# A two-layer kernel on one core: W2's first half through a split, a quarter of the up weights through an adding DMA, and one whole last store

## The chip, the core and the metric

The kernel runs on one core of a Trainium2 chip. The engines that matter are TensorE (PE, with its weight loads shown as PEld), VectorE (DVE), ScalarE (ACT), GpSimd (POOL) and SyncE (SP), which here only issues DMAs. The time is the device time of one execution in microseconds (us). Three runs of the kernel before gave 359.22, 359.46 and 359.85, so its median is 359.46 us.

## What is computed

The input x has 4 batches of 512 rows of 256 numbers, all in float32. Each of two layers does the same outer step with an inner pair of functions:

```
xn = layernorm(x);  s = mixer(xn);  g = silu(ffn(xn));  x = x + s * g

ffn(x):    up_gate = x @ W1.T;  up_lin = x @ W3.T          # W1, W3: 1024 x 256
           hidden  = fwht(silu(up_gate) * up_lin)          # Walsh-Hadamard over 1024, scaled
           return hidden @ W2.T                            # W2: 256 x 1024
mixer, layer 0: x + rmsnorm((g * (x @ W_in.T)) @ W_out.T) with one step of a recurrence from state zero
mixer, layer 1: causal attention with one head, then + x
```

The Hadamard transform is linear, so the kernel puts it on W2 once, and not on the hidden values of every batch.

## The kernel before

**Numbers in two parts.** A product of 512 columns in full float32 takes 0.86 us of PE here, one in float32r 0.233, so nearly all operands are split: a high part `hi` that float32r can hold, and the rest `lo`. `split` (L59 to L62) makes them with a copy on ACT and a subtraction, src minus hi, on DVE. `mm3` (L80) then needs three fast products for each full one: hi·lo, lo·hi and hi·hi.

**The weights of layer 0.** The up weights W1 and W3 come as four quarters of 512 KB, one tile of 128x1024 each. `load_w13` (L114) loads them by SP, and `split_w13` (L122) splits them; quarter 0 goes in two halves. Quarter q serves the hidden blocks 2q and 2q+1 of eight. W2 comes in two halves of 128x1024. `prep_w2` (L143) runs three butterfly stages on DVE (each is one addition and one subtraction of 128x512, L155 and L156), which do the Hadamard transform over the 8 blocks; a product with a 128x128 Hadamard matrix on PE does the rest, and its result in PSUM (`w2ps`) is split into `w2h` and `w2l`. The last butterfly result is split too, into `w2bh` and `w2bl`, and multiplied by `had`, the matrix in float32r, in four fast products. Half 0 of layer 0 is the exception ("native"): its last butterfly result goes to PE as full float32, in two products with the full float32 matrix `had_f`.

**Layer 0, batch by batch.** `ffn` (L466 to L561) takes hidden block c = 0 to 7 in turn: two groups of six products of 512 columns, the up-gate and up-linear parts `gu{c}_0` and `gu{c}_1` in PSUM; then a silu on ACT (L527) and a multiplication on DVE (L528, the "gate") give h; a split gives hh and hl. The down products (`dn`, 256 columns each) come later. In the first batch (`f0_0`), the high parts hh0 to hh3 are put into spare tiles (`early`), and the down products come after all the up products. The gu tiles rotate through a few PSUM banks, so a later group has to wait until silu and gate have read an earlier one.

**What stands beside it.** An object `Beside` (L884) gives out other work in slots of the batch's loop: for the first batch `prep_first` (L965: W2 of layer 0 and the product M of the mixer's two matrices, which scales `wout` into wgh and wgl, and splits `win`), then mixer and norm; for the second, W2 of layer 1 and the attention's weight products; for the third and fourth, the weights of layer 1 (`sraw` is loaded, combined, stored as `sw`, and loaded again) and the next norms. But this only says in which order the program is written. **The order on each engine in layer 0 is set by the tile framework's scheduler**, which moves independent instructions past each other from its own durations (L1197, `schedule_with_timeline_sim=True`), except where `issue_after` (`after(...)`, L463) ties one behind another. So an edit in one place can reorder all of layer 0. In layer 1 the order on PE is written out by hand (`line["fixed"]`, and the list `places` from L1083).

**Layer 1 and the end.** `ffn_s` (L563) does the same layer function with another scheme of half-size products. For the last batch, `gate_tile` (L1058) takes each of the four tiles of 128 rows as its down products end: silu on ACT, multiplication and addition on DVE (L1063, L1064), then a store. `first["last"]` ties the next tile's multiplication behind this tile's addition. Tiles 0 to 2 are stored whole by SP (L1066). Tile 3 is stored as 64 rows by SP and 64 rows by ACT (L1070).

The functions that the diff touches:

Of the kernel before, what the change touches and what calls it, by code (L numbers as in the profile page):

```python
# [11 lines left out]
F32 = mybir.dt.float32  # L12
# [9 lines left out]
P = 128  # L22
# [13 lines left out]
def kernel(ctx: ExitStack, tc: tile.TileContext, a: dict, out: bass.AP):  # L36
# [22 lines left out]
    def split(src, hi, lo, engine=nc.vector):  # L59

        h = nc.scalar.copy(hi, src)  # L61
        return h, engine.tensor_tensor(lo, src, hi.bitcast(F32), ALU.subtract)  # L62

    line = {"fixed": False, "last": None}
# [55 lines left out]
    def split_w13(layer, q, raw):  # L122
        both = wp.tile([P, 2, 2, S], F32R, tag="w13", name=f"w13_{layer}_{q}", bufs=4)
        hi, lo = both[:, 0], both[:, 1]
        if (layer, q) != (0, 0):
            split(raw, hi, lo)
            return hi, lo
        halves = [slice(c * D, (c + 1) * D) for c in range(2)]
        split(*(z[:, :, halves[0]] for z in (raw, hi, lo)))
        next(normed)  # L130
        with after(first["norm"][0]), after(first["norm"][1]):
            hi_, lo_ = split(*(z[:, :, halves[1]] for z in (raw, hi, lo)))
        first["w13"] = hi_, lo_
        return hi, lo
# [8 lines left out]
    def prep_w2(layer, raws, dst, scratch):  # L143

        w2h, w2l = dst
        for half in range(2):
            ds_ = slice(half * P, (half + 1) * P)
            cur = raws[half]  # L150
            for st, h in enumerate((1, 2, 4)):
                nxt = scratch(f"w2b{st}_{layer}_{half}", [P, NH, P])
                cv = cur.rearrange("p (g two h) d -> p g two (h d)", two=2, h=h)
                nv = nxt.rearrange("p (g two h) d -> p g two (h d)", two=2, h=h)
                nc.vector.tensor_tensor(nv[:, :, 0], cv[:, :, 0], cv[:, :, 1], ALU.add)  # L155
                nc.vector.tensor_tensor(nv[:, :, 1], cv[:, :, 0], cv[:, :, 1], ALU.subtract)  # L156
                cur = nxt
                yield

            native = layer == 0 and half == 0  # L160
            if not native:
                bh = t4(f"w2bh_{layer}_{half}", [P, NH, P], F32R)
                bl = t4(f"w2bl_{layer}_{half}", [P, NH, P], F32R)
                split(cur, bh, bl)
                yield
            for q in range(2):
                o = psum(f"w2ps_{layer}_{half}_{q}", [P, NH // 2, P])
                qs = slice(q * NH // 2, (q + 1) * NH // 2)
                if native:
                    matmul(o, had_f, cur[:, qs, :], start=True, stop=True)  # L170
                else:
                    matmul(o, had, bh[:, qs, :], start=True, stop=False)
                    matmul(o, had, bl[:, qs, :], start=False, stop=True)
                split(o, w2h[:, qs, ds_], w2l[:, qs, ds_])
                yield

# [289 lines left out]
    def ffn(name, xT, w13, w2, slot, defer=1, spare=(), parts=1, behind=False, tail=()):  # L466

        w2h, w2l = w2
        dn, outs, firsts = [], [], {}

        def down(c, hh, hl, tiles=range(NT)):
            if not dn:
                dn.extend(psum(f"{name}dn{i}", [P, 2, D], tag="dn", bufs=2) for i in range(2))
                outs.extend(dn[t // 2][:, t % 2, :] for t in range(NT))
            for t in tiles:
                o = outs[t]
                for n, (l, r) in enumerate(((hh, w2h), (hh, w2l), (hl, w2h))):  # L480
                    first = c == 0 and n == 0
                    stop = c == NH - 1 and n == 2

                    def one(start):
                        return matmul(
                            o, l[:, sl(t)], r[:, c, :], start=start, stop=stop, skip_group_check=True
                        )

                    if first and t % 2 == 1:
                        with tc.issue_after(firsts[t // 2].ins):
                            ins = one(False)
                    elif first:
                        ins = firsts[t // 2] = one(True)
                    else:
                        ins = one(False)
            return ins

        queue, gates, late = [], [], []  # L500
        for c in range(NH):
            with after(gates[-2] if behind and c >= 2 else None):
                wh, wl = w13(c // 2)
            gu = []
            for j in range(2):

                o = psum(f"{name}gu{c}_{j}", [P, S], **(DN[0] if behind and c == 1 else GU))
                cols = slice((c % 2) * D + j * P, (c % 2) * D + (j + 1) * P)
                gu.append((o, cols))
            for half in range(parts if c == 0 else 1):  # L510
                n = S // (parts if c == 0 else 1)
                ts_ = slice(half * n, (half + 1) * n)
                if parts == 1 or c:
                    for o, cols in gu:
                        last_up = mm3(o[:, ts_], k_pairs((wh, wl), cols, xT, ts_))
                    continue

                for n, (w, x) in enumerate(((wh, xT[0]), (wl, xT[0]), (wh, xT[1]))):
                    for o, cols in gu:
                        for k in range(2):  # L520
                            last_up = matmul(
                                o[:, ts_], w[:, k, cols], x[:, k, ts_],
                                start=n + k == 0, stop=n + k == 3,
                            )
            gu = [o for o, _ in gu]
            h = hid(f"{name}h{c}")
            first["silu"] = nc.scalar.activation(h, gu[0], AF.Silu)  # L527
            gates.append(nc.vector.tensor_tensor(h, h, gu[1], ALU.mult))  # L528
            first["gate"] = gates[-1]
            if c < len(spare):  # L530
                hh, hl = spare[c]
            else:
                hh = hid(f"{name}hh{c}", F32R)
                hl = hid(f"{name}hl{c}", F32R)
            if c < len(spare):
                nc.scalar.copy(hh, h)
                late.append((hl, h, hh))
            else:
                split(h, hh, hl)
            for _ in range(2 if c >= NH - 2 else 0):  # L540
                if late:
                    lo_, h_, hi_ = late.pop(0)
                    with after(gates[-1]):
                        nc.vector.tensor_tensor(lo_, h_, hi_.bitcast(F32), ALU.subtract)
            queue.append((c, hh, hl))
            ups = last_up if behind else None
            with after(gates[-1] if behind else None), after(ups):
                slot(2 * c)
            if len(queue) > defer:
                down(*queue.pop(0))  # L550
            with after(gates[-1] if behind else None), after(ups):
                slot(2 * c + 1)
        line["fixed"] = bool(tail)
        line["last"] = last_up
        for what in tail:
            what()
        for q in queue:

            with after(first.get("xt") if behind and q[0] >= NH - 2 else None):
                down(*q)  # L560
        return dn  # L561
# [403 lines left out]
    def prep_first():  # L965
        steps = prep_w2(0, raw2, w2, x_slot)
        with after(first["w13"][1]):
            next(steps)
        yield
        for _ in range(4):  # L970
            next(steps)
            yield
        with after(first["silu"]):
            nc.scalar.copy(had, had_f)
        for _ in range(2):
            next(steps)
            yield
        for _ in range(2):
            next(steps)
            yield  # L980
        load_x(1)
        product = prep_m(*raw_m)
        next(product)
        yield
        next(steps)
        yield
        next(product)
        yield
        yield from steps
# [68 lines left out]
    def gate_tile(t, o):  # L1058
# [2 lines left out]
        nc.scalar.activation(g, o, AF.Silu)  # L1061
        with after(first.get("last")):
            nc.vector.tensor_tensor(g, g, s, ALU.mult)  # L1063
        first["last"] = nc.vector.tensor_tensor(x, x, g, ALU.add)  # L1064
        if t + 1 < NT:
            nc.sync.dma_start(out[B - 1, sl(t), :], x)  # L1066
            return

        for queue, rows in ((nc.sync, slice(0, P // 2)), (nc.scalar, slice(P // 2, P))):
            queue.dma_start(out[B - 1, sl(t), :][rows], x[rows])  # L1070

    loaded = {}

# [127 lines left out]
```

## Time and profile before

| what | value |
|---|---|
| median of three runs | 359.46 us |
| the profiled execution's own time | 359.25 us |
| its span in the trace | 357.46 us (1.79 us lie outside) |
| PE busy | 350.7 us, 98% |
| PEld busy | 326.8 us, 91% |
| DVE busy | 287.2 us, 80% |
| ACT busy | 197.5 us, 55% |
| POOL busy | 20.8 us, 6% |
| first product of the up weights | 7.8 us |
| start of the last product | 352.21 us |
| last packet of the last store | 356.27 us |

The table's busy times come from the page of one profiled execution. A line of the timeline reads: start in us, length in us, engine, line, operation, out<-in, shape, number of instructions, and in brackets how long the engine was idle before it and who ended the wait. Instructions of one engine overlap by some 0.1 us in such lines: steps are therefore best measured from start to start. A product in full float32 shows as two records in the trace.

### The profile page before, as it was taken

To read this page: it belongs to the slowest core of one execution; us is meant where nothing else is said; L and a number is where in the kernel's file an instruction comes from. 1 tells how busy PE (TensorE), PEld (TensorE's weight loads), DVE (VectorE), ACT (ScalarE), POOL (GpSimd) and SP (SyncE) were. 2 spreads that over 40 slices of the span, in tenths; PEclk is the share of its full clock that TensorE was granted. 3 is DMA by queue.
4 is the path that set the end of the run, shared out by engine and by line. 5 is a ranking of instruction groups with operands and counts; after the bars stand their busy time and mean duration, and the time that the engine had idled before them with its cause. 6 is when DMAs were issued, how large, how long until landed. Compare 5 with 4: busy or idle time off the path is not lost.

```text
span 357.5 us, 6276 instructions
## 1 busy us (share of the span) xinstructions
PE 350.7 (98%) x2477; PEld 326.8 (91%) x2477; DVE 287.2 (80%) x597; ACT 197.5 (55%) x373; POOL 20.8 (6%) x22
## 2 busy tenths in 40 slices
PE   7999999999999999999999999999999999999994
PEld 5878998888988898888999999999999999999994
DVE  6899659998579938998887957989679897577645
ACT  4666166265463425674467745586455676555443
POOL 2000110300021110100100001100011000000000
PEclk9999999999999999999999999999999999999999
DMA  7935000301054316756257135662554635444401
GB/s 241 337 87 211 2 1 2 117 0 61 0 169 174 131 42 230 257 179 200 96 210 261 54 153 208 229 234 73 201 208 172 217 145 205 176 146 173 185 0 59
DMA packets 16300, 52.25 MB, mean 146 GB/s; under 512 B 1648, under 2 KB 7952, under 8 KB 16272
## 3 DMA queue, kind: packets, MB, share of 16 engines
q1 hardware_dynamic: 15904, 51.54, 40.9%
q8 instruction: 19, 0.31, 0.4%
q10 hardware_dynamic: 368, 0.33, 0.3%
q14 instruction: 9, 0.07, 0.1%
HBM read 42.40 MB, written 9.45 MB: 145 GB/s over the span
## 4 chain that ended last, share of the span: by engine, by line
PE 95%; DVE 3%; DMA 1%; ACT 0%; issue 0%; DVEq 0%
PE f_0dn L70 6%; PE f_1dn L70 6%; PE f_2dn L70 6%; PE f_0gu L70 6%; PE f_1gu L70 6%; PE f_2gu L70 6%; PE f_3gu L70 6%; PE f_3dn L70 5%; PE sc L70 4%; PE pv L70 4%; PE o L70 3%; PE v L70 3%; PE tq L70 3%; PE w2ps L70 1%; PE pt L70 1%; PE mps L70 1%
## 5 line engine op out<-in xcount | busy, mean ns | idle before, releaser
L70 PE MATMUL f_3gu<-xt,w 128*128 128x512 f32 x96 | 25.0, 396 | 0.0
L70 PE MATMUL f_2gu<-xt,w 128*128 128x512 f32 x96 | 24.8, 395 | 0.0
L70 PE MATMUL f_1gu<-xt,w 128*128 128x512 f32 x96 | 24.8, 395 | 0.0
L70 PE MATMUL f_0gu<-xt,w 128*128 128x512 f32 (+1 forms) x108 | 24.3, 378 | 0.0
L70 PEld LDWEIGHTS f_0gu<-xt,w 128*128 128x128 f32 x108 | 18.4, 188 | 4.6 <-issue 0.7
L70 PEld LDWEIGHTS f_1gu<-xt,w 128*128 128x128 f32 x96 | 17.0, 188 | 3.1
L70 PEld LDWEIGHTS f_2gu<-xt,w 128*128 128x128 f32 x96 | 17.0, 188 | 3.0
L70 PEld LDWEIGHTS f_3gu<-xt,w 128*128 128x128 f32 x96 | 17.0, 188 | 2.9
L61 ACT CAST f_2hh<-f_2h 128x512 fp32r<-128x512 f32 x16 | 10.0, 622 | 15.5 <-DVE f_2h L528 12.4
L70 PE MATMUL f_3dn<-w2l,f_3hh 128*128 128x256 f32 x64 | 17.7, 281 | 0.0
L70 PE MATMUL f_3dn<-w2h,f_3hh 128*128 128x256 f32 x64 | 17.7, 281 | 0.0
L70 PE MATMUL f_1dn<-w2l,f_1hh 128*128 128x256 f32 x64 | 17.7, 281 | 0.0
L70 PE MATMUL f_2dn<-w2h,f_2hh 128*128 128x256 f32 x64 | 17.7, 282 | 0.0
L70 PE MATMUL f_1dn<-w2h,f_1hh 128*128 128x256 f32 x64 | 17.6, 280 | 0.0
L70 PE MATMUL f_2dn<-w2l,f_2hh 128*128 128x256 f32 x64 | 17.6, 281 | 0.0
L70 PE MATMUL f_3dn<-w2h,f_3hl 128*128 128x256 f32 x64 | 17.0, 281 | 0.0
L70 PE MATMUL f_1dn<-w2h,f_1hl 128*128 128x256 f32 x64 | 17.0, 281 | 0.0
L70 PE MATMUL f_2dn<-w2h,f_2hl 128*128 128x256 f32 x64 | 16.7, 281 | 0.0
L61 ACT CAST f_3hh<-f_3h 128x512 fp32r<-128x512 f32 (+1 forms) x17 | 10.0, 594 | 10.1 <-DVE f_3h L528 5.9
L61 ACT CAST f_1hh<-f_1h 128x512 fp32r<-128x512 f32 x16 | 9.9, 622 | 9.7 <-DVE f_1h L528 6.6
L62 DVE TENSOR_TENSOR f_2hl<-f_2h,f_2hh 128x512 fp32r<-128x512 f32 x16 | 10.9, 684 | 4.5 <-ACT f_2hh L61 4.5
L62 DVE TENSOR_TENSOR f_3hl<-f_3h,f_3hh 128x512 fp32r<-128x512 f32 (+1 forms) x17 | 11.0, 654 | 3.7 <-ACT f_3hh L61 3.6
(487 smaller groups left out, 1145.9 us busy)
## 6 DMA issues: line engine op xcount, KB each, us to landing
sw<-s SPq DMA_DIRECT2D x32, 896.0 KB, 5.2
s<-sp SPq DMA_DIRECT2D x8, 512.0 KB, 4.3
s<-sp SPq DMA_DIRECT2D x8, 384.0 KB, 2.8
w2raw<-in_w SPq DMA_DIRECT2D x4, 512.0 KB, 5.6
sraw<-in_w SPq DMA_DIRECT2D x4, 512.0 KB, 3.6
mrb<-there SPq DMA_DIRECT2D x4, 512.0 KB, 3.7
w13raw<-in_w SPq DMA_DIRECT2D x3, 512.0 KB, 7.1
x<-in_x SPq DMA_DIRECT2D x3, 512.0 KB, 3.6
```

Of the source, the lines that this page charges most:

```text
L61: h = nc.scalar.copy(hi, src)
L62: return h, engine.tensor_tensor(lo, src, hi.bitcast(F32), ALU.subtract)
L70: ins = call(*args, **kwargs)
```

## The change

Three things are edited.

1. Half 0 of layer 0's W2 is no longer native. Its last butterfly result is split right after the last stage, in the same step, and four fast products replace the two full ones. The copy of the Hadamard matrix into `had` is written earlier in `prep_first` (after three steps of W2 and not after five).
2. Quarter 3 of the up weights is split in another way: ACT writes −src into the low part (`mul` by −1) and the high part as a copy, and then a DMA issued from POOL adds src into the low part. This is tied behind the third silu of the kernel; a list `first["silus"]` keeps the silus for that. What −src, rounded to float32r, leaves when src is added to it is the low part; DVE's subtraction for this quarter is gone.
3. In `gate_tile`, the tie of a multiplication behind the addition of the tile before is set only by tiles 2 and 3, and the last tile is stored whole by SP.

```diff
+    def split_by_dma(src, hi, lo):
+
+        nc.scalar.mul(lo, src, -1.0)
+        nc.scalar.copy(hi, src)
+        nc.gpsimd.dma_start(lo.bitcast(F32), src, accum_op=ALU.add)
...
         hi, lo = both[:, 0], both[:, 1]
-        if (layer, q) != (0, 0):
-            split(raw, hi, lo)
+        if q:
+            with after(first["silus"][2] if q == 3 else None):
+                (split_by_dma if q == 3 else split)(raw, hi, lo)
             return hi, lo
...
                 cur = nxt
-                yield
-
-            native = layer == 0 and half == 0
-            if not native:
-                bh = t4(f"w2bh_{layer}_{half}", [P, NH, P], F32R)
-                bl = t4(f"w2bl_{layer}_{half}", [P, NH, P], F32R)
-                split(cur, bh, bl)
-                yield
+                if st < 2 or layer or half:
+                    yield
+            bh = t4(f"w2bh_{layer}_{half}", [P, NH, P], F32R)
+            bl = t4(f"w2bl_{layer}_{half}", [P, NH, P], F32R)
+            split(cur, bh, bl)
+            yield
             for q in range(2):
                 o = psum(f"w2ps_{layer}_{half}_{q}", [P, NH // 2, P])
                 qs = slice(q * NH // 2, (q + 1) * NH // 2)
-                if native:
-                    matmul(o, had_f, cur[:, qs, :], start=True, stop=True)
-                else:
-                    matmul(o, had, bh[:, qs, :], start=True, stop=False)
-                    matmul(o, had, bl[:, qs, :], start=False, stop=True)
+                matmul(o, had, bh[:, qs, :], start=True, stop=False)
+                matmul(o, had, bl[:, qs, :], start=False, stop=True)
...
             first["silu"] = nc.scalar.activation(h, gu[0], AF.Silu)
+            first.setdefault("silus", []).append(first["silu"])
...
-        for _ in range(4):
+        for _ in range(2):
             next(steps)
             yield
         with after(first["silu"]):
             nc.scalar.copy(had, had_f)
-        for _ in range(2):
+        for _ in range(4):
             next(steps)
             yield
...
-        first["last"] = nc.vector.tensor_tensor(x, x, g, ALU.add)
-        if t + 1 < NT:
-            nc.sync.dma_start(out[B - 1, sl(t), :], x)
-            return
-
-        for queue, rows in ((nc.sync, slice(0, P // 2)), (nc.scalar, slice(P // 2, P))):
-            queue.dma_start(out[B - 1, sl(t), :][rows], x[rows])
+        ins = nc.vector.tensor_tensor(x, x, g, ALU.add)
+        if t > 1:
+            first["last"] = ins
+        nc.sync.dma_start(out[B - 1, sl(t), :], x)
```

## The prediction

> **What bounds the kernel now.** I read the shares first, then the chain, then 4 us windows of the first 40 us, where most of the change acts, and last the end.
>
> ```profile
> span 357.5 us, 6276 instructions
> ...
> PE 350.7 (98%) x2477; PEld 326.8 (91%) x2477; DVE 287.2 (80%) x597; ACT 197.5 (55%) x373; POOL 20.8 (6%) x22
> ...
> PE 95%; DVE 3%; DMA 1%; ACT 0%; issue 0%; DVEq 0%
> ```
>
> The chain of waits is TensorE (PE) for 95% of the span. In the timeline, from 7.8 us to the last matmul at 352.21, products follow each other at 0.233 us (512 columns) or 0.117 us (256) with no gap above 0.1 us except in the native W2 products. So a microsecond taken from PE is gained whole, and a microsecond for which PE waits anywhere before 352 is lost whole. Few waits can get shorter, and many could appear: what the other engines have in hand is the question.
>
> The windows of the start (columns: window, then busy us of PE, PEld, DVE, ACT, POOL with counts, granted clock, DMA share, GB/s):
>
> ```profile
> 16.00:20.00 4.00, 4.00 (x18) 2.88 (x17) 4.00 (x7) 3.69 (x7) 0.00 (x0) 1.00 0.33 94
> 20.00:24.00 4.00, 4.00 (x17) 2.92 (x16) 4.00 (x9) 1.71 (x3) 0.00 (x0) 1.00 0.33 95
> 24.00:28.00 4.00, 4.00 (x19) 3.22 (x18) 4.00 (x8) 3.29 (x7) 0.00 (x0) 1.00 0.56 167
> ```
>
> PE and VectorE (DVE) are both full. ScalarE (ACT) is 92% busy from 16 to 20 and 43% from 20 to 24. Each up product needs a PSUM bank that a silu on ACT or a gate on DVE has freed, so the order on these two decides whether PE starves.
>
> **Part 1: W2's first half from a split.** The PE timeline has one native product and six up products between two starts:
>
> ```profile
> 17.71 1.02 PE L70 MATMUL w2ps<-w2b,had_f 128*128 128x512 f32 x2
> 18.17 1.97 PE L70 MATMUL f_0gu<-xt,w 128*128 128x512 f32 x6
> 19.97 1.02 PE L70 MATMUL w2ps<-w2b,had_f 128*128 128x512 f32 x2
> ```
>
> 19.97 − 17.71 = 2.26, less 6 × 0.233 = 1.40, leaves 0.86 us for a native product. Two cost 1.72; the four that replace them 4 × 0.233 = 0.93: **−0.79**. The split adds a copy of 1024 to ACT (1.05, the w2bh row below) and a subtraction of 1024 to DVE (1.22).
>
> **Part 2: quarter 3 through an adding DMA.** DVE loses its subtraction of 1024 (1.22), so DVE's sum is unchanged; ACT gets one more pass of 1024 (the −src, 1.05). ACT has 2.1 us more in all. Average load would allow it. The order does not. In the changed program's order ACT has, after the second silu: third silu, −src, hi copy, w2bh copy, and only then the fourth silu. Steps from rows, start to start: 0.49 for a silu of 512 and 0.95 for a pass of 1024. The third silu starts at 16.69, so −src 17.18, copy 18.13, w2bh 19.08 to 20.13, fourth silu 20.03 (17.98 before).
>
> - gu4's first product waits for the gate of h2, which DVE ends at 19.14: PE has 0.1 to 0.2 us nothing to do. The first W2 product waits for w2bh: 20.21 against PE ready at 19.92, **0.3**. Together 0.4.
> - Further on, these rows of before stand in the way (ACT, then DVE):
>
> ```profile
> 24.71 1.05 ACT L61 CAST w2bh<-w2b 128x1024 fp32r<-128x1024 f32 x1 [0.88 <-DVE w2b L156]
> 25.66 0.62 ACT L61 CAST f_0hh<-f_0h 128x512 fp32r<-128x512 f32 x1
> 26.18 0.59 ACT L527 ACTIVATE f_0h<-f_0gu 128x512 f32<-128x512 f32 x1
> 26.76 1.71 ACT L202 ACTIVATE wgh<-wout,g 128x256 fp32r<-128x256 f32 x4
> ```
> ```profile
> 26.59 1.22 DVE L62 TENSOR_TENSOR w2bl<-w2b,w2bh 128x1024 fp32r<-128x1024 f32 x1
> ```
>
> The sixth silu (26.18) stands ahead of the four scalings of wgh. In the changed order it stands behind them, and both W2 high copies come just ahead of w2bh of half 1. From PE's second pair of W2 products at 24.18: w2h 24.61, w2h 25.10, w2bh 25.59, hh4 26.54, wgh 27.06 (1.61), silu 28.67 to 29.27, and gu6_1 reads on PE at 29.35. PE's work up to there is 16 × 0.233 = 3.74, so it would be ready at 27.92: **1.4** (0.3 of it shows earlier, before half 1's product with w2bl, which now waits for a copy that ends 26.64 plus 1.22 on DVE).
>
> Start together: **+1.8**, between 0 (if these waits are covered) and 1.95.
>
> **The adding DMA itself.** Before shows no DMA issued from GpSimd (POOL) and none that adds. The nearest rows are loads of the same 512 KB:
>
> ```profile
> sraw<-in_w SPq DMA_DIRECT2D x4, 512.0 KB, 3.6
> ...
> w13raw<-in_w SPq DMA_DIRECT2D x3, 512.0 KB, 7.1
> ```
>
> Single ones take 3.6 (alone) to 8.9 us (queued). Issued when −src is written, 18.2, it lands between 21.8 and 27.1. It is first read by the low-part products of gu6_0, about 26.8, and PE waits for the sixth silu until 29.35 anyway; a landing up to 28.2 costs nothing net. So by these rows it costs 0; nothing waits behind it on POOL before 40 us. Beyond about 10 us every microsecond counts whole. I take 0, and keep the late case as a rival.
>
> [...]
>
> **Later in layer 0.** The diff does not touch it, but the scheduler set a new order on all engines up to layer 1 (layer 1's is unchanged). I walked PE, ACT and DVE through the changed order with durations of before's rows.
>
> - f0_1: gu5_0 waits for the gate of h3. Between the gates of h0 and h3, DVE now has two more butterfly stages (four of 0.60 start to start), 17.36 us in all against 14.84 before; the gate ends 18.5 after gu0_0's last product, and PE has 56 × 0.117 + 49 × 0.233 = 17.97 in hand: **+0.6**.
> - f0_2: hl2 comes behind other work on DVE: **+0.3** (0 to 0.36).
> - f0_3: the queue of SP,
>
> ```profile
> 148.02 0.32 SPq L353 DMA_DIRECT2D sw<-s  x1
> 148.39 0.43 SPq L328 DMA_DIRECT2D sraw<-in_w  x1
> ```
>
> issues the last raw weights of layer 1 (sraw) behind the sw store of 148.02; now they come behind the next one, 155.92 in before. From gu5_1's last product: 0.43 + 0.42 to issue, 5.58 to land (this row's own), and 7.32 of DVE work on them and up to hl7: 13.83 with 0.08 to reach PE, against 36 × 0.233 + 38 × 0.117 and the last product's own 0.233, 13.07: **+0.8** (0 if it lands in 3.6; 1.2 if in 6.0).
>
> The same walk over before's own order gave 0.2 more than the trace has, so I take 0.2 off: **+1.5**, between 0 and 2.2.
>
> **The end.** DVE's four multiplies and four adds keep their durations (0.42); with the second multiply ahead of the first add its chain from the first to the last is 2.76 instead of 2.84: −0.08. The last store (rows of all engines' timeline):
>
> ```profile
> 351.95 1.92 SPq L1066 DMA_DIRECT2D out<-x  x3
> ...
> 353.89 0.42 DVE L1064 TENSOR_TENSOR x<-x,gl 128x256 f32<-128x256 f32 x1
> 354.34 0.55 SPq L1070 DMA_DIRECT2D out<-x  x1
> ```
>
> The whole stores ahead (128 rows, 0.33 each) have their last packet 1.35 us after issue (353.55 to 354.89). The two halves, issued together, took 0.55 each and end 1.93 after (354.34 to 356.27). One whole store: **−0.58**. SP is free. End together −0.66, between −0.7 and 0 (if a whole store that ends the program lands no sooner).
>
> **Sum:** −0.79 + 1.8 + 0 + 1.5 − 0.66 = **+1.85**. The profiled execution (359.25: span 357.46 and 1.79 around it) becomes 361.1. The median is 359.46, 0.2 above it: **361.3 us**.
>
> **The rivals.**
>
> - *Only the start waits.* The later waits are differences of large sums (17.97 against 18.5) and may be covered. For it: PE has no wait there in before. Then +1.85 − 1.5 = +0.35: 359.8, no measurable change.
> - *PE never waits: faster.* The place is the sixth silu. ACT has 2.3 us idle from 20 to 24, more than its 2.1 us of new passes. If the copies of w2h and w2bh slip into that time, because PE comes to the W2 products earlier than I walked it, the silu starts by 27.2 and PE's 3.74 us of work cover it; the small waits at 19 to 20 and the late ones, matters of order too, would be covered likewise. Price: −0.79 − 0.66 = −1.45: 358.0. It decides once all new waits together stay under 1.45 − 0.72 = 0.7 us. Against it: the W2 products' places on PE and the silu's behind wgh are in the program, and the durations on that path hardly vary.
> - *The adding DMA is late.* From about 10 us after 18.2 on, each microsecond goes to the time. 12 us would give +2: 363.3. [...] Against it: every other 512 KB needs under 9.
> - *The change does not do what it says*: DVE gets no relief, since w2bl costs what quarter 3 saves (1.22 each). That is so by the count, and stands in the sum as 0.
>
> **How the numbers follow.** Two runs differ measurably above some 0.2%, 0.72 us. Chances: the forecast 0.58, only the start 0.16, no waits 0.12, late DMA 0.12, other 0.02. Low end: the forecast with late waits of 0 and a little less at the start, 359.6. High end: with 2.2 late, 1.95 at the start, the end's gain halved and a DMA late by half a microsecond, 363.0. That leaves out the faster case and half of the late DMA, 0.18. Faster 0.12, within 0.2% 0.17 (the second case and a little of the forecast), slower 0.71.
>
> **What would show it.** In the profile after: no w2ps from had_f, four products at 0.23; PE idle 0.3 to 0.5 us around 19 to 20 and over 1 us before gu6_1, with the sixth silu behind wgh at about 28.7; the adding DMA landing before 28; PE gaps at gu5_0 in f0_1 (released by DVE's gate) and at the end of f0_3 (hl7); sraw3's issue after the sw of about 158; one last store, 1.35 us to its last packet. I am wrong if PE stays full through 30 us (then faster), or if its longest wait names a DMA from GpSimd (then slower than the range).

## The result, and the profile after

The changed kernel takes 361.83 us (median of six runs, 361.56 to 362.17), the kernel before 359.45 in as many. The ratio is 1.0068, with a 95% interval of 1.0058 to 1.0079: **2.4 us slower**. The prediction was 361.3 us, and slower.

The page of the changed kernel answers to the first lines shown of before:

```profile
span 360.4 us, 6286 instructions
...
PE 352.2 (98%) x2477; PEld 326.9 (91%) x2477; DVE 287.7 (80%) x597; ACT 199.4 (55%) x375; POOL 21.9 (6%) x23
...
PE 77%; DVE 12%; DMA 5%; ACT 3%; issue 2%; SPq 1%; DVEq 0%; ACTq 0%
```

PE is as busy as before by its share, and yet the chain of waits runs through PE for only 77% of the span, where it was 95%: DVE, DMA and ACT now release some of its work. The view of what PE waited for (us in total, times, longest) says where:

```profile
PE warm L76 <- DVE zr L935: 1.5, 1, 1.5
PE f_0gu L76 <- ACT f_0h L529: 0.8, 1, 0.8
PE f_3dn L76 <- DVE f_3hl L62: 0.8, 1, 0.8
PE f_1gu L76 <- DVE f_1h L531: 0.3, 1, 0.3
PE f_2dn L76 <- DVE f_2hl L62: 0.2, 1, 0.2
```

The first stands in the kernel before too. The other four are new: one at the start (a silu), and one in each later batch of layer 0 (DVE's gate, hl2 and hl7). They are the places that the prediction named. The lengths here count from the modelled end of the product ahead; from start to start of products, less the product's own 0.233 or 0.117, the new waits are longer, and there are seven: 0.25, 0.19, 0.28 and 1.10 us behind the products that start at 18.9, 20.0, 27.7 and 28.2 us, then 0.42 behind that of 73.3, 0.40 behind 114.9 and 0.95 behind 171.9.

ACT's timeline at the start:

```profile
19.29 1.06 ACT L61 CAST w2bh<-w2b 128x1024 fp32r<-128x1024 f32 x1
20.24 0.59 ACT L529 ACTIVATE f_0h<-f_0gu 128x512 f32<-128x512 f32 x1
...
25.86 1.07 ACT L61 CAST w2bh<-w2b 128x1024 fp32r<-128x1024 f32 x1
26.81 0.63 ACT L61 CAST f_0hh<-f_0h 128x512 fp32r<-128x512 f32 x1
27.33 1.71 ACT L204 ACTIVATE wgh<-wout,g 128x256 fp32r<-128x256 f32 x4
28.94 0.58 ACT L529 ACTIVATE f_0h<-f_0gu 128x512 f32<-128x512 f32 x1
```

The sixth silu begins at 28.94 behind the four scalings (walked: 28.67), and the PE timeline shows what waits for it:

```profile
28.24 0.50 PE L76 MATMUL w2ps<-w2bl,had 128*128 128x512 f32 x1
29.58 0.72 PE L76 MATMUL f_0gu<-xt,w 128*128 128x512 f32 x2 [0.83 <-ACT f_0h L529]
```

The adding DMA was in time, in the list of issues (KB each, us to landing):

```profile
w<-w13raw POOLq DMA_DIRECT2D x1, 512.0 KB, 5.4
```

It was issued at 18.76, so it landed at 24.2; gu6_0 began at 26.3. And the end: the last store is issued at 357.78 and lands 1.7 us later, where the halves of before took 2.0 and 2.3 (its last packet comes 1.35 us after the issue, as predicted):

```profile
out<-x SPq DMA_DIRECT2D x1, 128.0 KB, 1.7
```

### The profile page after: what moved, and what is told of

It reads as the page before. It is cut to its first block, busy times and chain, and to the rows that moved or that the text cites. A ratio compares the mean times of both kernels' runs of the same rounds, so it can differ in the third digit from the quotient of the medians.

```text
span 360.4 us, 6286 instructions
## 1 busy us (share of the span) xinstructions
PE 352.2 (98%) x2477; PEld 326.9 (91%) x2477; DVE 287.7 (80%) x597; ACT 199.4 (55%) x375; POOL 21.9 (6%) x23
## 4 chain that ended last, share of the span: by engine, by line
PE 77%; DVE 12%; DMA 5%; ACT 3%; issue 2%; SPq 1%; DVEq 0%; ACTq 0%
PE f_0dn L76 6%; PE f_2dn L76 5%; PE f_1dn L76 5%; PE f_3dn L76 5%; PE f_3gu L76 5%; PE sc L76 4%; PE pv L76 4%; PE f_1gu L76 3%; PE v L76 3%; PE f_2gu L76 3%; PE tq L76 2%; DMA w2raw<-in_w 2%; PE o L76 2%; DMA sraw<-in_w 2%; DVE w2b L162 1%
## 5 line engine op out<-in xcount | busy, mean ns | idle before, releaser
L76 PE MATMUL f_2gu<-xt,w 128*128 128x512 f32 x96 | 24.2, 394 | 0.0
```

Source lines behind the costliest of these rows:

```text
L76: ins = call(*args, **kwargs)
```

## The experiments

**Theory:** the work that the change adds and removes is worth little; the new waits come from the order that the scheduler gives to ACT, DVE and SP after each edit. **Rivals:** the waits come from ACT's two more passes of 1024 and the adding DMA beside a full DVE (4.00 of 4 us from 20 to 24), whatever the order; or only one of the parts brings them all.

### Each part alone

Part 3 alone (the diff's last hunk on the kernel before).

> The kernel before with part 3 alone (the new order at the end and the whole last store). Layer 0 keeps its order. Theory, each part costs what its own waits cost and the end gains by itself: -0.08 for the order on DVE and -0.55 for the store, so 358.8 us, the last packet some 1.35 us after the issue of the last store. Rival, a whole store at the program's end lands no sooner than two halves: -0.1 us, 359.35.

Measured: 358.48, ratio 0.9980 (0.9970 to 0.9989). The gain of the end is there by itself, 0.8 us, 0.2 more than expected. On DVE the last addition begins at 353.76 and not at 353.89, with PE as before.

The store alone:

```diff
         first["last"] = nc.vector.tensor_tensor(x, x, g, ALU.add)
-        if t + 1 < NT:
-            nc.sync.dma_start(out[B - 1, sl(t), :], x)
-            return
-
-        for queue, rows in ((nc.sync, slice(0, P // 2)), (nc.scalar, slice(P // 2, P))):
-            queue.dma_start(out[B - 1, sl(t), :][rows], x[rows])
+        nc.sync.dma_start(out[B - 1, sl(t), :], x)
```

> The kernel before with the last store whole by SP, and the order of the multiplies and adds as before. Theory: of the 0.8 us that the whole of part 3 took off, 0.6 to 0.7 are the store's, so -0.65, 358.7 us, and about 1.35 us from its issue to its last packet. Rival, the order on DVE carries it: -0.1 us, 359.2.

Measured: 358.82, ratio 0.9985 (0.9976 to 0.9993), so 0.5 us (0.25 to 0.86). In its trace the stretch from the last product's start to the end is 0.61 shorter (5.25 to 4.64). Most of part 3's gain is the store; what is left for the order on DVE, 0.3, is not clear of the intervals' width.

Part 1 alone (the hunks in `prep_w2` and `prep_first`):

> The kernel before with part 1 alone: W2's first half from a split, quarter 3 still split with DVE. Theory, what counts is the order that each edit leaves on ACT and DVE: PE loses 0.79 of work, and by a walk over this kernel's order PE waits about 3.3 us within 18 to 37 us (largest 1.7 for a low part of W2 near 36 us, none later than that in layer 0), and 0.1 us more after each of five waits: +3.0, about 362.4 us. Rival, the split is the gain and the adding DMA brings all the waits: 358.7 us with PE full.

Measured: 361.43, ratio 1.0059 (1.0046 to 1.0072). The waits of PE in it:

```profile
PE f_0dn L70 <- DVE w2l L62: 1.3, 1, 1.3
PE mps L70 <- ACT wih L61: 0.4, 1, 0.4
PE f_0dn L70 <- ACT w2h L61: 0.2, 1, 0.2
```

The rival falls: the split alone costs 2.1 us. From start to start the three waits are 0.39, 0.61 and 1.51, between 31 and 36 us. DVE has 1.22 us more to do where it was full, and the low part of W2 comes late; since DVE's work grew, this run alone does not tell order from load. PE's work fell by 0.79. There is no wait after 40 us. The expectation was 0.9 too high: two of the five waits (at 18 and 29 us) were only 0.03 and 0.04, and the largest was 1.5 and not 1.7.

Part 2 alone (`split_by_dma`, the tie, and `first["silus"]`):

> The kernel before with part 2 alone: quarter 3 through the adding DMA, W2's first half native. Theory: one wait of 0.3 us at the start, and the three late waits of layer 0 (about 0.4, 0.4 and 0.95 us as in the changed kernel), 0.1 us more after each: +2.3, about 361.8 us; so the late waits come with this part. Rival, the late waits come from part 1, since it takes work from PE and leaves DVE its own: +0.4, 359.85 us, no wait of PE after 40 us.

Measured: 361.23, ratio 1.0054 (1.0041 to 1.0067).

```profile
PE f_1gu L78 <- DVE f_1h L538: 0.3, 1, 0.3
PE f_2dn L78 <- DVE f_2hl L62: 0.2, 1, 0.2
PE f_3dn L78 <- DVE f_3hl L62: 0.2, 1, 0.2
```

The three late waits come with this part, and the start has none above 0.1; the change is +1.9 and not +2.3. From start to start they are 0.42, 0.40 and 0.34. The third is 0.6 shorter than in the changed kernel, and so is the time of its load: from sraw's issue (158.24 here, 159.80 there) to the first sum that waits for it, it is 5.2 us here and 5.8 there. The rows, here and in the changed kernel:

```profile
163.46 0.43 DVE L342 TENSOR_TENSOR ssum<-sraw 128x256 f32<-128x256 f32 x1 [1.27 <-DMA sraw<-in_w]
```
```profile
165.64 0.42 DVE L335 TENSOR_TENSOR ssum<-sraw 128x256 f32<-128x256 f32 x1 [1.89 <-DMA sraw<-in_w]
```

The edit moves nothing in batches 1 to 3 by itself; the scheduler does. The parts do not add up: −0.8, +2.1 and +1.9 make +3.2, and all three together +2.4.

### The order alone

One tie more in the changed kernel, all work the same:

```diff
         nc.scalar.mul(lo, src, -1.0)
-        nc.scalar.copy(hi, src)
+        with after(first["w2b"][0][0]):
+            nc.scalar.copy(hi, src)
...
-            split(cur, bh, bl)
+            first.setdefault("w2b", []).append(split(cur, bh, bl))
```

> The changed kernel with one tie more: ACT's copy of quarter 3's high part is tied behind the copy w2bh of half 0, so these two change places. The work is the same. The scheduler then puts the sixth silu ahead of the wgh scalings again, and the order later in layer 0 comes out near that of before. Theory, the waits come from the order and not from the work: one wait of 0.2 us near 19 us and some below 0.1, none in later layer 0; -0.85 against before, about 358.6 us. Rival, the waits come from ACT's two more passes and from the adding DMA beside a full DVE: the wait before gu6_1 stays near 1 us and the time above 360.5.

Measured: **357.89**, ratio 0.9963 (0.9950 to 0.9975): 1.4 us faster than the kernel before, 0.6 more than expected, and some 3.8 faster than the changed one (by the two ratios). The only wait of PE that the view lists is the one that every kernel here has:

```profile
PE warm L77 <- DVE zr L936: 1.5, 1, 1.5
```

ACT's timeline shows why; the sixth silu stands ahead of the scalings:

```profile
18.36 1.04 ACT L61 CAST w2bh<-w2b 128x1024 fp32r<-128x1024 f32 x1
19.29 1.05 ACT L68 CAST w<-w13raw 128x1024 fp32r<-128x1024 f32 x1
...
27.03 0.61 ACT L530 ACTIVATE f_0h<-f_0gu 128x512 f32<-128x512 f32 x1
27.52 1.70 ACT L205 ACTIVATE wgh<-wout,g 128x256 fp32r<-128x256 f32 x4
```

On PE the tie also moved half 1's product with w2bl (28.24 in the changed kernel) behind the next six up products, to 29.19, so its wait of 0.28 is gone too. With the same work in hand, neither ACT's 2.1 us more nor the adding DMA is what costs. The gain is also the size of the prediction's faster rival (−1.45), reached by order. It beats both kernels.

Another way to the same: two steps of the side work change places.

```diff
         product = prep_m(*raw_m)
-        next(product)
-        yield
         next(steps)
         yield
+        next(product)
+        yield
```

> The changed kernel with two steps of the side work written in the other order: the step of W2's half 1 ahead of the one that scales wgh. The work is the same. The scheduler then puts the sixth silu ahead of the wgh scalings, but keeps quarter 3's two passes ahead of w2bh. Theory: the waits of 0.25 and 0.2 near 19 to 20 us stay (and 0.1 after each), those of 0.3 and 1.1 before gu6_1 go, and so do the three late ones; some 0.7 us above the kernel with the tie of w2bh: about 358.6 us. Rival, the late waits come with quarter 3's passes standing ahead of w2bh: they stay, and the time is about 360.4.

Measured: 358.43, ratio 0.9973 (0.9963 to 0.9983). The waits before gu6_1 and the three late ones are gone, and one of 0.18 at 19.8 stays; the one of 0.25 ahead of it is gone too. It is some 0.4 to 0.5 us above the kernel with the tie, and the two intervals overlap. The theory holds, but for the wait of 0.25, and the size within 0.2.

One of the late waits by itself:

```diff
-        nc.sync.dma_start(raw, a["w13_1"][q])
+        first["sraw"] = nc.sync.dma_start(raw, a["w13_1"][q])
...
-            nc.sync.dma_start(parts[i].bitcast(F32), sdram[q][i])
+            with after(first["sraw"]):
+                nc.sync.dma_start(parts[i].bitcast(F32), sdram[q][i])
```

> The changed kernel with one tie more: every sw store-back load of layer 1's weights is tied behind the load of sraw3 on SP, so sraw3 is issued again where the kernel before has it. The start is untouched. Theory, the third late wait (0.95 us for hl7 and 0.1 after it) comes from the place of this one load: it vanishes, and 1.05 us less than the changed kernel, about 360.8 us; the waits at the start and in batches 1 and 2 stay. Rival, hl7 is late because DVE has too much in the fourth batch, whenever the load lands: the time stays at 361.8.

Measured: 360.76, ratio 1.0037 (1.0024 to 1.0051), 1.07 below the changed kernel. The wait at the end of batch 3 is gone, and those at 73 and 115 us stay at 0.42 and 0.41. The place of one load on SP cost 1.05 us. SP's timeline in the changed kernel, against 148.02 and 148.39 before:

```profile
150.51 9.19 SPq L355 DMA_DIRECT2D sw<-s  x2
159.80 0.38 SPq L330 DMA_DIRECT2D sraw<-in_w  x1
```

The two issues of sw are one line here (the second ends at 159.70); sraw follows them.

### How much cover the adding DMA has

Quarter 3 later, in the changed kernel:

```diff
-            with after(first["silus"][2] if q == 3 else None):
+            with after(first["silus"][4] if q == 3 else None):
```

> The changed kernel with quarter 3's part tied behind the fifth silu in place of the third, so -src ends and the adding DMA is issued near 23.4 us and not 18.7. Theory, the DMA takes 5.4 us from issue to landing as in the changed kernel, and once it is late each microsecond counts whole: it lands near 29, PE waits some 2.5 us for it before gu6_0, and no other wait of more than 0.2 us is left, since the order on ACT comes out better: about 1.1 us above the kernel before, 360.4 us. Rival, PE has so much other work in hand there that the landing is covered: no wait there, 357.9 us.

Measured: 362.56, ratio 1.0084 (1.0071 to 1.0097). The expectation was 2.2 too low, and the rival (no wait) falls. The place is right:

```profile
PE f_0gu L76 <- DMA w<-w13raw: 3.1, 1, 3.1
```

The DMA was issued at 24.09 and landed 5.8 later; PE's pause is 3.2, not 2.5, and there is no other. But this execution took 361.49, and the other four 362.39 to 362.88, with a granted clock of 0.992 to 0.995 for the core, where the profiled one had 0.999. About half of the miss lies in this difference; no trace of one of the four shows what it is.

The adding DMA twice, in the kernel with the tie:

```diff
-        nc.scalar.mul(lo, src, -1.0)
+        nc.scalar.mul(lo, src, -2.0)
...
-        nc.gpsimd.dma_start(lo.bitcast(F32), src, accum_op=ALU.add)
+        for _ in range(2):
+            nc.gpsimd.dma_start(lo.bitcast(F32), src, accum_op=ALU.add)
```

> The kernel with the tie of w2bh (357.9 us, PE without a wait), with the adding DMA issued twice, one after the other, on the same tile; ACT writes -2 src, so quarter 3's low part comes out twice what it should be. Theory: one adding DMA takes 5.4 us and has cover until the low part is read near 26.8, so the first is free; the second lands near 29 and PE waits about 2 us for it before gu6_0, and 0.1 after it: 2.1 above that kernel, 360.0 us. Rival, the cover is larger than I think, since PE has other products there: no wait, 357.9.

Measured: 364.55, ratio 1.0141 (1.0126 to 1.0156), 6.7 us above the kernel with the tie, not 2.1. The mechanism is there (by the view PE waits 4.9 us in one piece for that DMA) and both sizes are wrong. Windows (busy us of PE, PEld, DVE, ACT, POOL, then the granted clock, DMA share, GB/s):

```profile
24.00:28.00 4.00, 2.57 (x12) 1.73 (x10) 4.00 (x8) 3.72 (x8) 0.86 (x1) 1.00 0.86 244
28.00:32.00 4.00, 0.55 (x1) 0.50 (x2) 3.53 (x7) 1.83 (x4) 0.00 (x0) 0.59 0.99 261
32.00:36.00 4.00, 4.00 (x12) 3.12 (x11) 0.00 (x0) 0.00 (x0) 0.00 (x0) 0.55 0.73 262
36.00:40.00 4.00, 4.00 (x22) 3.42 (x21) 3.20 (x6) 2.98 (x6) 0.00 (x0) 1.00 0.01 3
```

The second DMA, issued at 24.13, ran beside the loads of x and W2 on SP (DMA share 0.86 to 0.99) and took 7.3 us; PE paused 5.0, from 26.4 to 31.45. The granted clock fell while PE paused. If it fell from 1.00 to 0.50, the lowest mean in the windows of this run and the next, the means of 1.00, 0.59, 0.55 and 1.00 put the fall at 28.7 us, 2.3 after PE stopped, and the return at 35.6. From 31.45 to 35.5 the products of 512 columns follow each other at 0.427 us and not at 0.233: nine steps, which cost 1.9 us, the slower first one (0.59 us) among them. 5.0 + 1.9 is the 6.7 within the spread of single executions.

Three times:

> The same with three adding DMAs and -3 src (low part of quarter 3 three times what it should be). Theory: the third lands near 34.5; the scheduler puts some of PE's other work ahead, and PE waits about 3.6 us for it in one piece and 1.5 in two other places: 5.4 above the kernel with the tie, 363.3 us. In the kernel with quarter 3 tied behind the fifth silu, where PE waited 3.2 us in one piece, four of five runs were 1 us longer than the profiled one and had a granted clock of 0.992 to 0.995; if a pause of more than some 3 us brings that, this one shows it too: granted clock under 0.996 and 1 us or more on top, 364 to 365. Rival, that clock has to do with something else: clock 0.997 or more, 363.3.

Measured: 367.19, ratio 1.0224 (1.0203 to 1.0244). This is 2 to 3 us above the expectation with the clock in it: PE paused 0.72, 0.54 and 5.78, the long pause 2.2 more than was said. The clock is down again after it:

```profile
32.00:36.00 4.00, 0.70 (x2) 0.61 (x3) 0.58 (x1) 0.00 (x0) 0.00 (x0) 0.67 0.69 131
36.00:40.00 4.00, 4.00 (x13) 3.22 (x12) 1.67 (x3) 0.60 (x1) 0.00 (x0) 0.50 0.71 262
40.00:44.00 4.00, 4.00 (x27) 3.64 (x27) 3.96 (x10) 1.61 (x3) 0.00 (x0) 0.98 0.00 0
```

Its five runs have a granted clock of 0.985 to 0.989. By the same working as above it was down from 33.35 to 40.2 us, 6.8 us where the run before has 6.9; PE's pause ends at 35.30. After the pauses of 0.7 and 0.5 the clock stayed at 1.00, in both windows from 24 to 32 us.

## Why the prediction was right

By the profiled executions the span grew from 357.46 to 360.36, 2.90. From the same two traces, term by term:

| term | predicted | measured |
|---|---|---|
| PE's work, two native products for four | −0.79 | −0.79 |
| waits at the start | +1.8 | 0.25 + 0.19 + 0.28 + 1.10 = +1.82 |
| adding DMA | 0 | 0 (landed 24.2, read from 26.3 on) |
| f0_1, f0_2, f0_3 | 0.6 + 0.3 + 0.8, less 0.2 = +1.5 | 0.42 + 0.40 + 0.95 = +1.77 |
| further steps 0.1 too long | not in the sum | 7 × 0.10 to 0.11 = +0.73 |
| the end | −0.66 | −0.64 (last product's start to the end, 5.25 to 4.61) |
| sum | +1.85 | +2.89 |

By the medians the change is +2.38. The profiled execution of the changed kernel is the longest of its six (362.17), and that of before lies 0.2 under its median, so 0.5 of the 2.90 is the spread of single executions. The sum is therefore 1.04 short of its own traces; that the forecast, 361.3, is only 0.5 from the median is in part luck.

- **What bounds the kernel** held: each wait of PE came out in the time, and where no wait was (the kernel with the tie), the gain was what PE's work and the end gave.
- **The start** held in place, releaser and size. The step that carried it was to write down ACT's order, and not its load: averaged over the 4 us windows ACT had room.
- **The adding DMA** held: 5.4 us, between the two rows that bounded it (3.6 and 8.9), and 4.5 to 7.3 in the other runs. Whether DVE held it up no run here shows. DVE was full beside it (5.44 us of 5.44), and with DVE 42% busy from 30.7 to 35.2 us (the third of three DMAs) it still took 4.5. DVE's own subtraction of 1024 took 1.22 us beside it, as before.
- **The later waits** held in place and releaser. The step that failed is the 0.2 taken off since the walk had given that much too much for before's own order: without it the sum of the three, 1.7, is 0.07 from the 1.77 of the trace. That it is so near is luck: the three miss by −0.18, +0.10 and +0.15, and these cancel. For f0_1 the prediction's own figures, 18.5 less 17.97, give 0.53 and not 0.6. The third goes with the time of one load, 5.58 us in the walk and 5.8 in the trace (it was 5.2, with a wait of 0.34, with part 2 alone). In f0_1, DVE has six stages of W2 between the gates of h0 and h3, where before has four. Gates and one of the stages, changed kernel, then before:

```profile
56.44 0.69 DVE L531 TENSOR_TENSOR f_1h<-f_1h,f_1gu 128x512 f32<-128x512 f32 x1 [1.37 <-ACT f_1h L529]
...
60.30 0.69 DVE L162 TENSOR_TENSOR w2b<-w2b 128x512 f32<-128x512 f32 x1
60.91 0.68 DVE L163 TENSOR_TENSOR w2b<-w2b 128x512 f32<-128x512 f32 x1
61.51 0.68 DVE L531 TENSOR_TENSOR f_1h<-f_1h,f_1gu 128x512 f32<-128x512 f32 x1
...
73.08 0.68 DVE L531 TENSOR_TENSOR f_1h<-f_1h,f_1gu 128x512 f32<-128x512 f32 x1
```
```profile
56.20 0.69 DVE L528 TENSOR_TENSOR f_1h<-f_1h,f_1gu 128x512 f32<-128x512 f32 x1 [0.79 <-ACT f_1h L527]
...
70.36 0.68 DVE L528 TENSOR_TENSOR f_1h<-f_1h,f_1gu 128x512 f32<-128x512 f32 x1
```

  From the gate of h0 (56.44) to the start of h3's gate it is 16.64, against 14.16 in before (56.20 to 70.36): 2.5 us more, as walked.
- **A cost was left out:** seven steps were 0.10 to 0.11 us longer than their product's own 0.233 or 0.117. Six of them follow one of the new waits, and the one at 15.6 us follows a product that is 0.03 late; in sum they are a quarter of the 2.90. This is the larger part of what the sum is short of.
- **The end** held: the store alone gave 0.5 by its medians and 0.61 in its trace, where 0.58 was said.
- **The rivals:** "PE never waits" was wrong for this order, and right for the work: a single tie gave its 1.4 us. "The adding DMA is late" was wrong in this kernel, and its price was too low where it came true: with pauses of 5.0 and 5.8 us the time paid for the pause and for a stretch of products at half the clock behind it.

## What to carry to other kernels

Where one engine is full from end to end, an edit elsewhere is priced by the order that it leaves on the engines that feed the full one, read instruction by instruction; busy shares only say that there may be room. If a scheduler sets the order, look at the places far from the edit too (here half of the late loss came from the place of one load on SP, the other half, by the rows of the trace, from DVE's order in two batches), and try a tie before giving up a change: the same work was 2.4 us slower or 1.4 us faster. The adding DMA cost nothing where it landed at 24.2 us ahead of a first reader at 26.3, and 3.2 us of PE where it landed at 29.9 behind it; so count such a transfer's cover from issue to its first reader, with the other transfers of that time running.

## What was not expected of the hardware

After a pause of PE at full clock (0.19, 0.25, 0.40, 0.42, 0.95 and 1.10 us in the changed kernel, 3.2 with quarter 3 later) the second product started 0.10 to 0.11 us late, whatever the pause. It also did after a product that was only 0.03 late (at 15.6 us in the changed kernel). The cause stays open.

With pauses of 5.0 and 5.8 us the granted clock of PE fell within the pause, 2.3 and 3.8 us after its start, to a mean of 0.50 in the window from 36 to 40 us of the second, and came back 6.9 and 6.8 us later; PE worked in 4.1 and 4.9 us of that, and in the first the products of 512 columns took 0.427 us where they take 0.233. After 1.1 us it did not fall (1.000 in the changed kernel); after 3.2 it did not in the profiled execution (1.00 in every window from 20 to 60 us), and the four others of that kernel were 1 us longer at a clock of 0.992 to 0.995. What decides whether the clock falls, and for how long, no run here shows.

One such stretch, 6.8 us at half, would lower the mean clock of 361 us by 0.009, an estimate from the windows above. The four longer runs lie 0.004 to 0.007 under the profiled one of their kernel, so less than one stretch each, and the runs of the kernel before spread from 0.996 to 1.000 by themselves; no trace of one of the four shows a fall.
